# The adjacency of a graph network read for four tiles at a time, in pieces of 512 bytes, and its masks made one pair earlier

## The chip, the cores and the metric

The kernel runs on one core of one Trainium2 chip. The metric is the device time in microseconds (us), the median of the runs shown; lower is better. The core has five engines: TensorE (PE; the load of its weights is listed apart as PEld), VectorE (DVE), ScalarE (ACT), GpSimd (POOL) and SyncE (SP). Here SP issues the loads and POOL the stores; both are carried out by the core's 16 DMA engines.

## The reference

Two layers of a graph neural network on 2708 nodes with 1024 features, float32, with one adjacency matrix `adj` (2708 x 2708, int32, some 1% ones):

```python
# layer 0
h = jnp.maximum(_layernorm(x), 0.0)
f = h @ Wf + bf
g = h @ Wg + bg
e = jax.nn.relu(f @ g.T)
scores = jnp.where(adj > 0, e, NEG)          # NEG = -9e15
x = x + jax.nn.softmax(scores, axis=1) @ (h @ W + bW)
# layer 1
h = jnp.maximum(_layernorm(x), 0.0) @ W1
e = jax.nn.leaky_relu(h @ a1 + (h @ a2).T, 0.2)
e = jnp.where(adj > 0, e, NEG)
x = x + jax.nn.relu(jax.nn.softmax(e, axis=1) @ h)
```

Both layers need the mask of `adj`: 0 where there is an edge, a large negative number where there is none.

## The kernel before, in words

The rows of the score matrix are worked off in five panels `p`, of 576, 576, 532, 512 and 512 rows (`width`). Scores are held transposed: the neighbours are on the 128 partitions, the panel's rows run along the free dimension. The neighbours are cut into 20 full tiles of 128, taken as 10 pairs `q`, and what is left over (two partial tiles, MONO and TINY) is an eleventh unit, LEFT. Every full tile consists of four runs of 32 nodes that lie 128 apart; the two tiles of a pair are neighbours in `adj`, so that a row of it holds 64 consecutive numbers (256 bytes) for a pair in each of four places.

The large products are done with seven half-size products in place of eight (M1 to M7, Strassen's scheme in Winograd's form). For layer 0, `f @ g.T` is folded into `h @ (Wf Wg^T) @ h.T`: for each panel `project_q` makes the left side B, and `scores(p, B)` (L1382 to L1512) multiplies it with the tiles of `h`, which come as tiles `As` from `hs_d`, a buffer in DRAM. In panel 0 the tiles for it are only just being made: `make_until(q + 2)` sees to the units that the loop needs next, from x by way of `hsT`, whose parts are stored to `hs_d` by POOL. Then follow softmax, `aggregate` (the attention times `h`), and `project` with W; the panels follow each other, with the next panel's `project_q` between its scores and the aggregation of the one before.

The masks are made in panels too, by the three functions that `mask_maker(p)` returns (L783 to L840). `fetch(q)` loads the pair's adjacency: four DMAs into `adj_i`, each of 32 partitions x 16 blocks x 256 bytes (512 KB in all), and, in panels 0 to 2 whose width is over 512, four more into `adj_t` for the panel's tail of up to 64 rows. `convert(q)` turns the integers into bf16 values 0 or minus a large number, `nm`, in one VectorE operation, or two on ACT (`by_act`: the loop of panels 1 to 4). `turn(q, k)` turns the 32x32 squares of one tile with VectorE's transpose into its half of `mask`, and with k = 1 stores the pair's mask to `mk_d`, from where layer 1 reads it. `finish` (in `scores`) takes `mask` for layer 0 from the on-chip memory.

The pair's work is spread over the loop of `scores`. In step q stand `fetch(q + 2)` (L1436 to L1437), `convert(q + 1)` after product M5, `turn(q + 1, 0)` after M2 and `turn(q + 1, 1)` after M7. What a panel needs before its loop is made by `first_masks(p, step)` (L844 to L853), which is hung into the products ahead of it: those of `project_q` for panel 0 (M1, M2, M7), of `project` for panels 1 to 3 (M1, M5, M7) and of `aggregate` for panel 4 (M2, M6, M7).

What sets the order: `load` (L137) issues every load on SP in program order, so a load that has to wait holds up those behind it. `store` (L141) issues on POOL. SP's DMAs use eight completion semaphores in turn. `adj_i`, `As`, `x`, `w` and `hc` are taken in order from one ring of 12 stream buffers (`stream`, L127), and a buffer is free when the last reader of its former content, a store included, is done; `adj_t`, `nm`, `mask` and the score tiles come from 54 slots (`slot`). In the scores VectorE keeps the order of the program (`nc.hold`). Work of other stages is dealt out between products by `behind(rate)`.

Of the kernel before, what the change touches and what calls it, by code (L numbers as in the profile page):

```python
# [9 lines left out]
BF = mybir.dt.bfloat16  # L10
I32 = mybir.dt.int32
# [7 lines left out]
P = 128  # L19
W = 512  # L20
B32 = 32
# [36 lines left out]
def kernel(  # L58
# [19 lines left out]
    nc = InOrder(tc)  # L78
# [12 lines left out]
    F = W // P  # L91
# [20 lines left out]
    LEFT = NQ  # L112
    units = pairs + [(MONO, TINY)]
    order_of_units = [(q, k) for k in range(2) for q in range(NQ)] + [(LEFT, 0), (LEFT, 1)]
    WX, HX = width[0], width[0] // 2
# [9 lines left out]
    def slot(name, shape=(P, WX), dt=FP):  # L125
        return slots.tile(list(shape), dt, tag="slot", name=name)

    def stream(name, shape=(P, D), dt=FP):
        return strm.tile(list(shape), dt, tag="strm", name=name)

    def in_16(o, i):

        n = o.shape[0]
        k = n // 16 * 16
        return [(o, i)] if n in (k, 1) or not k or i.shape[0] != n else [(o[:k], i[:k]), (o[k:], i[k:])]

    def load(o, i):  # L137
        for a, b in in_16(o, i):
            tc.keep_in_program_order(nc.sync.dma_start(a, b))

    def store(o, i):  # L141
        for a, b in in_16(o, i):
            nc.gpsimd.dma_start(a, b)  # L143

    def bank(name, shape=(P, W), dt=FP):
        return psum.tile(list(shape), dt, tag="bank", name=name)
# [26 lines left out]
    mk_d = [dram.tile([P, NQ + 1, 2, width[p]], BF, name=f"mk_d{p}") for p in range(NP)]  # L173
# [109 lines left out]
    def add(o, a, b):  # L283
        nc.vector.tensor_tensor(o, a, b, OP.add)
# [91 lines left out]
    def sums_h():  # L376

        def fetch(q, two):
            i, j = group_of[q]
            for m in (M1, M2):  # L380
                two.append(stream("hr", (P, 2, W)))
                (load if "m" in got else by_scalar)(two[-1], hg_d[i][:, m:m + 2, j])

        def first(q, two):
            (a0, a1), (b0, b1) = ((t[:, 0], t[:, 1]) for t in two)
            add(b1, a1, b1)
            sub(a1, a0, a1)

        def second(q, two):
            (a0, a1), (b0, b1) = ((t[:, 0], t[:, 1]) for t in two)  # L390
            sub(a0, b1, a0)
            sub(b0, b0, a0)
            i, j = group_of[q]
            store(hg_d[i][:, M6:M7 + 1, j], two[0])
            store(hg_d[i][:, M3, j], b0)
            store(hg_d[i][:, M5, j], b1)
            summed[0] += 1
        for q in range(NQ):
            two = []
            put(1.4, lambda q=q, two=two: held(first, q, two), lambda q=q, two=two: fetch(q, two), ready=lambda: sums_may[0])  # L400
            put(1.4, lambda q=q, two=two: held(second, q, two), ready=lambda: sums_may[0])
# [34 lines left out]
    c0 = consts.tile([P, 1], FP, name="c0")  # L436
# [98 lines left out]
    def make_until(q):  # L535
        while min(q, NQ - 1) not in made:
            one()
# [113 lines left out]
    for name, gs in (("pick_lo", (0, 1)), ("pick_hi", (0, 2, 3))):  # L651
        t = consts.tile([P, P], FP, name=name)
# [128 lines left out]
    mk_sb = {}  # L781

    def mask_maker(p):  # L783

        r0, w = base[p], width[p]
        NG, NB = P // B32, W // B32
        tail = -(-(w - W) // B32)
        raw, neg = {}, {}

        def columns(q):  # L790

            if q < LEFT:
                return [[start_of_tile(t) + P * g for g in range(NG)] for t in pairs[q]]
            return [[base[g // 2] + W + g % 2 * B32 for g in range(NG)], [base[2] + W] * NG]

        def fetch(q):
            a = stream("adj_i", (P, NB, 2, B32), I32)
            b = slot("adj_t", (P, tail, 2, B32), I32) if tail else None
            raw[q] = a, b
            c0, c1 = columns(q)  # L800

            def square_rows(t, blocks, g, k, r, j, n):
                load(t[B32 * g:B32 * (g + 1), :, k] if k is not None else
                     t[B32 * g:B32 * (g + 1)].rearrange("p b k c -> p b (k c)"),
                     adj[r:r + blocks * B32, j:j + n].rearrange("(b r) j -> r b j", r=B32))
            for t, blocks, r in ((a, NB, r0), (b, tail, r0 + W)):
                for g in range(NG if t is not None else 0):
                    if q < LEFT:
                        square_rows(t, blocks, g, None, r, c0[g], 2 * B32)
                    else:  # L810
                        for k, c in enumerate((c0, c1)):
                            square_rows(t, blocks, g, k, r, c[g], B32)

        def convert(q, by_act=False):
            a, b = raw.pop(q)
            neg[q] = []
            for t, blocks in ((a, NB), (b, tail)):
                if t is not None:
                    m = slot("nm", (P, 2, blocks, B32), BF)
                    if by_act and t is a:  # L820
                        nc.scalar.activation(m, t.rearrange("p b k c -> p k b c"), AF.Sign, bias=minus_half)
                        nc.scalar.activation(m, m, AF.Identity, bias=minus_big, scale=BIG / 2)
                    else:
                        nc.vector.tensor_scalar(m, t.rearrange("p b k c -> p k b c"), 0.0, -BIG, op0=OP.is_le, op1=OP.mult)
                    neg[q].append(m)

        def turn(q, k):
            if k == 0:
                mk_sb[p, q] = slot("mask", (P, 2, WX), BF)
            mk = mk_sb[p, q]  # L830
            m = neg[q]
            nc.vector.transpose(mk[:, k, :W].rearrange("p (s g r) -> p g s r", s=F, g=NG),
                                m[0][:, k].rearrange("p (g s) c -> p g s c", g=NG))
            if tail:
                nc.vector.transpose(mk[:, k, W:W + tail * B32].rearrange("p (b r) -> p b r", r=B32), m[1][:, k])
            if k == 1:
                neg.pop(q)
                store(mk_d[p][:, q], mk[:, :, :w])

        return fetch, convert, turn  # L840

    makers = [mask_maker(p) for p in range(NP)]

    def first_masks(p, step):  # L844
        fetch, convert, turn = makers[p]
        if step == 0:
            fetch(0)
            fetch(1)
        elif step == 1:
            convert(0)  # L850
        else:
            turn(0, 0)
            turn(0, 1)  # L853

    def load_mask(p, q, k):
        mt = slot("maskl", (P, WX), BF)
# [525 lines left out]
    def scores(p, B):  # L1382

        w = width[p]
        h = w // 2
        lo, hi = slice(0, h), slice(h, w)
        fetch, convert, turn = makers[p]
# [44 lines left out]
        for q in range(NQ):  # L1432
            n = P
            make_until(q + 2)
            rate = 1.3 if NQ - 1 not in made else rates[p]
            if q + 2 <= LEFT:  # L1436
                fetch(q + 2)  # L1437
            if p == 0 and q == NQ - 2:
                ahead[0] = 2
                sums_h()  # L1440
            if p in ORDERED and q in (2, 6):
                (copy_residual if q == 2 else bias_residual)(p)
            sa, sb = slot("Sa"), slot("Sb")
            S[pairs[q][0]], S[pairs[q][1]] = sa, sb
            X, Y, Z = (bank(f"s{k}") for k in "xyz")
            m1, t = slot("sm1"), slot("st")
            product(q, M1, X, True)
            for s in (lo, hi):
                add(m1[:n, s], X[:n, :h], rb[:n, s])
            if left_over:  # L1450
                left_over()
            product(q, M6, Z, True)
            add(t[:n, lo], Z[:n, :h], m1[:n, hi])
            behind(rate, True)
            product(q, M5, Y, True)
            add(t[:n, hi], Y[:n, :h], m1[:n, hi])
            if q + 1 <= LEFT:
                convert(q + 1, p > 0)
            behind(rate, True)
            product(q, M2, X, False)  # L1460
            add(sa[:n, lo], X[:n, :h], rb[:n, lo])
            if q + 1 <= LEFT:
                turn(q + 1, 0)
            behind(rate, True)
            product(q, M7, Z, False)
            add(sb[:n, hi], Z[:n, :h], t[:n, hi])
            if q + 1 <= LEFT:
                turn(q + 1, 1)
            behind(rate, True)
            product(q, M3, Y, False)  # L1470
            add(sa[:n, hi], Y[:n, :h], t[:n, lo])
            finish(q, sa, 0)
            behind(2 * rate, True)
            left_over = lambda q=q, sb=sb, Z=Z, m1=m1: last(q, sb, Z, m1)
# [6 lines left out]
        t = stream("As", (P, 2, NH, P))  # L1481
# [408 lines left out]
    for p in range(NP):  # L1890
# [6 lines left out]
        g = aggregate_quartered(p, S, sm, next_right, then, fine=1.0) if p else aggregate(1, p, S, sm, then, rate=4.0)  # L1897
# [34 lines left out]
```

## Time and profile before

| | |
|---|---|
| Median of 3 runs | 3057.45 us (3056.61 to 3057.47) |
| The profiled execution | 3054.54 us |
| Its span, first to last instruction | 3052.8 us |
| Mean granted TensorE clock | 0.996 |
| TensorE busy | 3000.2 us, 98% of the span |
| VectorE / ScalarE / GpSimd busy | 67% / 18% / 16% |
| DMA | 766.80 MB in 448065 packets, mean 251 GB/s |
| Packets under 512 bytes | 175488 |
| `adj_i` loads of 128 KB on SP | 200 |
| Scores of panel 0 | from 210 to 379 us |

How to read it: the span is cut up by engine. A row such as "PE sx L1407 <- DMA As<-hs_d" says that TensorE, before the instruction of line 1407 that writes `sx`, stood idle until the DMA that loads `As` from `hs_d` had landed. The tiles are called by the program's names. Idle time of an engine that is not the bottleneck costs nothing by itself. The windows give, for a stretch of time, the busy time of each engine, the granted clock, and the share of the 16 DMA engines' time that was taken.

### The profile page before, as it was taken

Reading aid. Unit: us, or ns where it says so; the run is one execution under the profiler, and the core shown is the slowest. Engines: PE = TensorE matmul, PEld = TensorE weight load, DVE = VectorE, ACT = ScalarE, POOL = GpSimd, SP = SyncE. Lnnn points to the kernel's source line nnn. Section 1 sums busy time; section 2 is a strip of 40 time slices with the busy share of each in tenths; the row PEclk is TensorE's granted clock in tenths of the full one; section 3 lists DMA queues with packets and bytes.
Section 4 is the critical chain, followed back from the end, with each engine's and each line's share of the span. In section 5 each row is a group of like instructions: output and inputs, shape, how many; then the busy total and the mean of one; then the engine's idle time right before and its main releaser. Section 6 shows DMA issues by size and latency. Waiting matters only on the chain.

```text
span 3052.8 us, 41716 instructions
## 1 busy us (share of the span) xinstructions
PE 3000.2 (98%) x14642; PEld 2297.9 (75%) x14642; DVE 2043.3 (67%) x4578; ACT 545.6 (18%) x888; POOL 495.9 (16%) x770
## 2 busy tenths in 40 slices
PE   8999999999999999999999999999999999999999
PEld 5576777667877588885888886784767959879695
DVE  5776794575751586616965276867978768887863
ACT  3420020021200121101211011302222131212200
POOL 1421111210112110214111011131212010020201
PEclk9999999999999999999999999999999999999999
DMA  6989978887466786757967588689768768878797
GB/s 227 304 259 271 302 274 306 263 276 237 159 237 156 226 255 218 250 156 245 281 204 256 164 232 274 220 295 340 240 211 261 268 207 292 291 267 295 256 304 269
DMA packets 448065, 766.80 MB, mean 251 GB/s; under 512 B 175488, under 2 KB 262304, under 8 KB 447824
## 3 DMA queue, kind: packets, MB, share of 16 engines
q1 hardware_dynamic: 387696, 584.80, 59.7%
q0 software_dynamic: 54464, 164.78, 16.2%
q10 hardware_dynamic: 5696, 14.55, 1.4%
q8 instruction: 116, 1.90, 0.2%
q14 instruction: 93, 0.76, 0.1%
HBM read 630.04 MB, written 138.11 MB: 252 GB/s over the span
## 4 chain that ended last, share of the span: by engine, by line
PE 70%; issue 12%; DVE 11%; DMA 3%; POOL 2%; ACT 1%; SPq 1%; POOLq 0%; DVEq 0%; ACTq 0%
PE gy L678 6%; PE gz L678 6%; PE gz L1096 5%; PE sz L1407 5%; PE gx L678 5%; PE pz L1296 4%; PE px L1296 4%; PE py L1296 3%; PE sx L1407 3%; PE sy L1407 3%; PE gx L1096 3%; PE gy L1096 3%; PE M_ps L591 3%; PE gv L678 3%; DVE P L45 2%
## 5 line engine op out<-in xcount | busy, mean ns | idle before, releaser
L1407 PE MATMUL sz<-B,As 128*128 128x288 f32 (+2 forms) x1200 | 292.9, 393 | 6.9 <-DVE st L45 4.5
L1407 PEld LDWEIGHTS sz<-B,As 128*128 128x128 f32 x1200 | 227.8, 190 | 56.5 <-DVE st L45 8.0
L1407 PE MATMUL sx<-B,As 128*128 128x288 f32 (+2 forms) x800 | 202.6, 397 | 7.5 <-DMA As<-hs_d 5.6
L1407 PE MATMUL sy<-B,As 128*128 128x288 f32 (+2 forms) x800 | 199.9, 393 | 0.5 <-DMA As<-hs_d 0.5
L678 PE MATMUL gz<-Sa,hc 128*128 128x288 f32 (+2 forms) x800 | 185.8, 392 | 0.0
L1407 PEld LDWEIGHTS sx<-B,As 128*128 128x128 f32 x800 | 153.3, 192 | 41.8 <-issue 4.6
L1407 PEld LDWEIGHTS sy<-B,As 128*128 128x128 f32 x800 | 152.3, 191 | 31.9 <-DMA As<-hs_d 0.9
L678 PEld LDWEIGHTS gz<-Sa,hc 128*128 128x128 f32 x800 | 151.6, 190 | 32.2 <-issue 2.2
L1096 PE MATMUL gz<-quarter,hc 128*128 128x128 f32 (+2 forms) x1344 | 168.8, 279 | 3.8 <-DVE gT L45 3.7
L1096 PEld LDWEIGHTS gz<-quarter,hc 128*128 128x128 f32 x1344 | 160.6, 191 | 5.0 <-DVE gT L45 4.5
L143 POOL DMA_DIRECT2D out_dram<-x_res x164 | 80.9, 500 | 470.8 <-DVE x_res L45 460.6
L1296 PE MATMUL py<-w,ps 128*128 128x512 f32 x320 | 142.1, 593 | 0.4 <-DMA w<-wt_d 0.4
L1296 PE MATMUL pz<-w,ps 128*128 128x512 f32 x320 | 142.0, 594 | 0.0
L1296 PE MATMUL px<-w,gT 128*128 128x512 f32 x320 | 141.1, 593 | 0.0
L143 POOL DMA_DIRECT2D mk_d<-mask x55 | 35.9, 653 | 516.3 <-DVE mask L45 510.4
L1296 PEld LDWEIGHTS pz<-w,ps 128*128 128x128 f32 x320 | 60.2, 190 | 76.2 <-issue 71.9
L678 PE MATMUL gy<-T,hc 128*128 128x288 f32 (+2 forms) x480 | 113.6, 398 | 3.9 <-DMA hc<-hg_d 3.9
L1296 PEld LDWEIGHTS py<-w,ps 128*128 128x128 f32 x320 | 60.4, 190 | 75.8 <-issue 71.9
L1296 PEld LDWEIGHTS px<-w,gT 128*128 128x128 f32 x320 | 60.1, 190 | 71.3 <-issue 66.9
L591 PE MATMUL M_ps<-wgT,wfT 128*128 128x512 f32 x256 | 111.8, 593 | 1.6 <-ACT hsT L45 1.6
L678 PEld LDWEIGHTS gy<-T,hc 128*128 128x128 f32 x480 | 92.2, 192 | 24.4 <-DMA hc<-hg_d 4.4
L45 ACT ACTIVATE P<-P 128x576 f32<-128x576 f32 (+3 forms) x111 | 72.0, 650 | 207.3 <-DVE P L45 207.2
(391 smaller groups left out, 5830.6 us busy)
## 6 DMA issues: line engine op xcount, KB each, us to landing
hc<-hg_d SPq DMA_DIRECT2D x175, 512.0 KB
As<-hs_d SPq DMA_DIRECT2D x150, 512.0 KB
hc<-hr_d SPq DMA_DIRECT2D x119, 512.0 KB
hc<-hs_d SPq DMA_DIRECT2D x112, 512.0 KB
w<-wt_d SPq DMA_DIRECT2D x96, 512.0 KB
w<-in_L_gnn_W_dram SPq DMA_DIRECT2D x72, 512.0 KB
md<-md_d SPq DMA_DIRECT2D x56, 512.0 KB
adj_i<-in_adj_dram SPq DMA_DIRECT2D x200, 128.0 KB
```

The costliest lines, as they stand in the source:

```text
L45: i = f(*a, **k)
L143: nc.gpsimd.dma_start(a, b)
L591: nc.tensor.matmul(ps, wfT[a][c // NH][:, c % NH, :], wgT[b][c], start=(c == 0), stop=(c == NC - 1))
L678: nc.tensor.matmul(ps[d], left(m, k, d), right(m, k), start=(start and k == 0), stop=(k == K - 1), skip_group_check=True)
L1096: nc.tensor.matmul(ps[:, d], lhs[:, d * P:(d + 1) * P], inner_right(m, n, k), start=(start and k == 0 and d == 0), stop=(k == NK - 1), ski ...
L1296: nc.tensor.matmul(ps, left[i][m][:, k, :], w_[k], start=(start and k == 0), stop=(k == NH - 1), skip_group_check=True)
L1407: nc.tensor.matmul(ps[:n, :h], lefts[q][:, i % 2, c, :n], B[m][c // 2][:, c % 2, :h], start=(start and c == 0), stop=(c == NH - 1), skip_g ...
```

## The change

A unit n below LEFT is no longer a pair but half of the panel's first 512 rows (n even: the first 256; n odd: the others) for four tiles, the pairs n - n % 2 and the next one. A row of `adj` holds 128 consecutive numbers, 512 bytes, for them in each of the four places, so a fetch has four DMAs of 32 partitions x 8 blocks x 512 bytes, again 512 KB. The tail is loaded with odd n, for four tiles at once. `convert` has as many elements as before, with a tail in odd n alone, which is twice as wide. `turn(n, j)` fills half of the rows of the two tiles of one pair, in two transposes of 128x256 in place of one of 128x512, and with odd n does the tail as well. The masks of two pairs are complete after the odd unit and are stored then. LEFT is done as before.

All of it stands one pair further ahead: step q of the loop fetches unit q + 3 and converts and turns unit q + 2. `first_masks` therefore makes two units: step 1 converts and turns unit 0 and fetches unit 2, step 2 converts and turns unit 1. Over a panel the same bytes are read, converted and turned. Since one more unit is converted ahead of the loop, panels 1 to 4 have nine conversions by ACT in place of ten.

```diff
-        def fetch(q):
-            a = stream("adj_i", (P, NB, 2, B32), I32)
-            b = slot("adj_t", (P, tail, 2, B32), I32) if tail else None
...
+        def fetch(n):
+            parts = NG if n < LEFT else 2
+            h = n % 2 if n < LEFT else 1
+            nb = NB // 2 if n < LEFT else NB
+            a = stream("adj_i", (P, nb, parts, B32), I32)
+            b = slot("adj_t", (P, tail, parts, B32), I32) if tail and h else None
+            raw[n] = a, b
+            c0, c1 = columns(n // 2 * 2 if n < LEFT else n)
...
-            for t, blocks, r in ((a, NB, r0), (b, tail, r0 + W)):
+            for t, blocks, r in ((a, nb, r0 + (h * W // 2 if n < LEFT else 0)), (b, tail, r0 + W)):
                 for g in range(NG if t is not None else 0):
-                    if q < LEFT:
-                        square_rows(t, blocks, g, None, r, c0[g], 2 * B32)
+                    if n < LEFT:
+                        square_rows(t, blocks, g, None, r, c0[g], P)
...
-        def turn(q, k):
-            if k == 0:
-                mk_sb[p, q] = slot("mask", (P, 2, WX), BF)
-            mk = mk_sb[p, q]
-            m = neg[q]
-            nc.vector.transpose(mk[:, k, :W].rearrange("p (s g r) -> p g s r", s=F, g=NG),
-                                m[0][:, k].rearrange("p (g s) c -> p g s c", g=NG))
...
+        def squares(mk, k, m, at, gs):
+            nc.vector.transpose(mk[:, k, :W].rearrange("p (s g r) -> p g s r", s=F, g=NG)[:, gs],
+                                m[0][:, at].rearrange("p (g s) c -> p g s c", s=F))
+            if tail and len(m) > 1:
+                nc.vector.transpose(mk[:, k, W:W + tail * B32].rearrange("p (b r) -> p b r", r=B32), m[1][:, at])
+
+        def turn(n, j):
+            m = neg[n]
...
+                h, q = n % 2, n // 2 * 2 + j
+                if h == 0:
+                    mk_sb[p, q] = slot("mask", (P, 2, WX), BF)
+                for k in range(2):
+                    squares(mk_sb[p, q], k, m, 2 * j + k, slice(2 * h, 2 * h + 2))
+                done = h == 1
+            if j == 1:
+                neg.pop(n)
+            if done:
+                store(mk_d[p][:, q], mk_sb[p, q][:, :, :w])
...
         if step == 0:
             fetch(0)
             fetch(1)
-        elif step == 1:
-            convert(0)
-        else:
-            turn(0, 0)
-            turn(0, 1)
+            return
+        convert(step - 1)
+        turn(step - 1, 0)
+        turn(step - 1, 1)
+        if step == 1:
+            fetch(2)
...
-            if q + 2 <= LEFT:
-                fetch(q + 2)
+            if q + 3 <= LEFT:
+                fetch(q + 3)
...
-            if q + 1 <= LEFT:
-                convert(q + 1, p > 0)
+            if q + 2 <= LEFT:
+                convert(q + 2, p > 0)
...
-            if q + 1 <= LEFT:
-                turn(q + 1, 0)
+            if q + 2 <= LEFT:
+                turn(q + 2, 0)
...
-            if q + 1 <= LEFT:
-                turn(q + 1, 1)
+            if q + 2 <= LEFT:
+                turn(q + 2, 1)
```

More of the change, by code (lines that the diff above doesn't have):

```diff
@@ L794, in columns, with square_rows @@
             return [[base[g // 2] + W + g % 2 * B32 for g in range(NG)], [base[2] + W] * NG]
-        def fetch(q):
-            a = stream("adj_i", (P, NB, 2, B32), I32)
-            b = slot("adj_t", (P, tail, 2, B32), I32) if tail else None
-            raw[q] = a, b
-            c0, c1 = columns(q)
-            def square_rows(t, blocks, g, k, r, j, n):
+        def fetch(n):
[6 more added lines that the diff above has]
+            c0, c1 = columns(n // 2 * 2 if n < LEFT else n)
+            def square_rows(t, blocks, g, k, r, j, m):
                 load(t[B32 * g:B32 * (g + 1), :, k] if k is not None else
                      t[B32 * g:B32 * (g + 1)].rearrange("p b k c -> p b (k c)"),
-                     adj[r:r + blocks * B32, j:j + n].rearrange("(b r) j -> r b j", r=B32))
-            for t, blocks, r in ((a, NB, r0), (b, tail, r0 + W)):
+                     adj[r:r + blocks * B32, j:j + m].rearrange("(b r) j -> r b j", r=B32))
+            for t, blocks, r in ((a, nb, r0 + (h * W // 2 if n < LEFT else 0)), (b, tail, r0 + W)):
                 for g in range(NG if t is not None else 0):
-                    if q < LEFT:
-                        square_rows(t, blocks, g, None, r, c0[g], 2 * B32)
+                    if n < LEFT:
+                        square_rows(t, blocks, g, None, r, c0[g], P)
                     else:
@@ L812, in fetch, with convert @@
                             square_rows(t, blocks, g, k, r, c[g], B32)
[L814 to L817, printed above, removed]
+        def convert(n, by_act=False):
+            a, b = raw.pop(n)
+            neg[n] = []
+            for t in (a, b):
                 if t is not None:
-                    m = slot("nm", (P, 2, blocks, B32), BF)
+                    blocks, parts = t.shape[1:3]
+                    m = slot("nm", (P, parts, blocks, B32), BF)
                     if by_act and t is a:
@@ L824, in convert @@
                         nc.vector.tensor_scalar(m, t.rearrange("p b k c -> p k b c"), 0.0, -BIG, op0=OP.is_le, op1=OP.mult)
-                    neg[q].append(m)
-        def turn(q, k):
-            if k == 0:
-                mk_sb[p, q] = slot("mask", (P, 2, WX), BF)
-            mk = mk_sb[p, q]
-            m = neg[q]
-            nc.vector.transpose(mk[:, k, :W].rearrange("p (s g r) -> p g s r", s=F, g=NG),
-                                m[0][:, k].rearrange("p (g s) c -> p g s c", g=NG))
[L834 to L838, printed above, removed]
+                    neg[n].append(m)
+        def squares(mk, k, m, at, gs):
[5 more added lines that the diff above has]
+            m = neg[n]
+            if n == LEFT:
+                if j == 0:
+                    mk_sb[p, n] = slot("mask", (P, 2, WX), BF)
+                squares(mk_sb[p, n], j, m, j, slice(0, NG))
+                q, done = n, j == 1
+            else:
+                h, q = n % 2, n // 2 * 2 + j
[8 more added lines that the diff above has]
+                store(mk_d[p][:, q], mk_sb[p, q][:, :, :w])
         return fetch, convert, turn
```

## The prediction

> **What bounds the kernel now.** I read the page first: the busy times say what can be won at all, then who stands before whom.
>
> ```profile
> span 3052.8 us, 41716 instructions
> PE 3000.2 (98%) x14642; PEld 2297.9 (75%) x14642; DVE 2043.3 (67%) x4578; ACT 545.6 (18%) x888; POOL 495.9 (16%) x770
> DMA packets 448065, 766.80 MB, mean 251 GB/s; under 512 B 175488, under 2 KB 262304, under 8 KB 447824
> ```
>
> TensorE is busy for 3000.2 of 3052.8 us, and the change touches no matmul (in the built program its order is the same). So at most 52.6 us of idle time, and whatever slow clock that brings, is to be had. The list of TensorE's waits says where the idle time stands:
>
> ```profile
> PE sx L1407 <- DMA As<-hs_d: 5.6, 3, 2.8
> ...
> PE sz L1407 <- DVE st L45: 4.5, 6, 1.5
> ...
> PE sx L1486 <- DMA As<-hsl_d: 2.3, 1, 2.3
> PE sz L1407 <- DMA As<-hs_d: 2.3, 1, 2.3
> ...
> PE py L1296 <- DMA w<-wt_d: 0.4, 1, 0.4
> ```
>
> Columns: total, times, longest. The four DMA rows, with 0.5 more at sy, are waits for transfers that share the 16 DMA engines with the adjacency. By TensorE's timeline all but the `w` row fall in the scores of panel 0 (210 to 379 us):
>
> ```profile
> 237.78 3.14 PE L1407 MATMUL sz<-B,As 128*128 128x288 f32 x8 [2.32 <-DMA As<-hs_d]
> 240.72 2.87 PE L1407 MATMUL sy<-B,As 128*128 128x288 f32 x8
> 246.10 2.29 PE L1407 MATMUL sx<-B,As 128*128 128x288 f32 x4 [2.52 <-DMA As<-hs_d]
> 279.51 3.87 PE L1407 MATMUL sx<-B,As 128*128 128x288 f32 x8 [2.78 <-DMA As<-hs_d]
> ```
>
> Call the stalls A (237.78), B (246.10), C (279.51): 7.62 us. Around them groups of eight matmuls take 3.14, 2.87, 3.66 and 3.87 us where 2.10 is usual, 5.1 us more, at a lower granted clock. The windows show that clock, and the DMA engines full:
>
> ```profile
> 170.00:190.00 20.00, 20.00 (x84) 15.66 (x83) 8.13 (x18) 3.37 (x7) 2.85 (x6) 1.00 0.75 250
> 190.00:210.00 20.00, 20.00 (x95) 16.00 (x93) 14.85 (x31) 3.87 (x7) 3.76 (x7) 1.00 0.83 271
> 210.00:230.00 20.00, 20.00 (x94) 15.90 (x92) 16.45 (x42) 4.42 (x10) 4.51 (x8) 1.00 0.95 232
> 230.00:250.00 20.00, 15.16 (x58) 11.14 (x57) 15.55 (x38) 5.10 (x9) 4.86 (x9) 0.83 0.91 324
> 250.00:270.00 20.00, 20.00 (x93) 15.99 (x92) 16.74 (x38) 2.05 (x4) 3.44 (x6) 1.00 1.00 246
> 270.00:290.00 20.00, 17.22 (x64) 12.93 (x63) 9.49 (x20) 0.00 (x0) 0.55 (x1) 0.91 0.91 248
> ```
>
> The last three columns are clock, DMA share, GB/s. From 210 to 290 the share is 0.91 to 1.00. The wait list of SP's queue for 195 to 370 tells why As is late:
>
> ```profile
> SPq L139 <- DMA hs_d<-hsT: 23.4, 4, 11.3
> SPq L139 <- DMA hg_d<-hr: 17.3, 4, 10.1
> ```
>
> SP stands up to 11.3 us for a stream buffer whose last content must first be stored; those stores land that late because the engines are full. So two things bound A, B and C in series: the stores' landing and the DMA rate under it.
>
> [...] 342 GB/s per full share from 379 to 641 (284 / 0.83, almost no adj), 306 from 641 to 780 (248 / 0.81). [...] Here a stall of 2.3 us already brought slow groups.
>
> **The change part by part.**
> *Packets.* The 139 us from 641 to 780 at 0.81 are 1801 engine-us; 28.4 MB of other traffic at 21.4 B/ns (342 / 16) take 1327, which leaves 474 for some 26000 small packets: 18 ns each. A fetch with its tail has 2304 of them: 42 engine-us, 2.6 us of all 16 engines. At 21.4 B/ns a 512-byte piece takes 24 ns at best, [...] with its share of tail a fetch becomes 27 to 33 engine-us. Saved: 0.6 to 0.95 us of the full engines per step. In panel 0 that counts. In panels 1 to 4 TensorE doesn't wait for As at all, so 6 to 8 us of DMA time per panel are hidden there by TensorE itself; bare, they would be worth that much.
>
> *Lookahead.* Fetch, convert and transposes move one pair forward. SP issues fetch(2) of panel 0 before the x loads, 16 adj DMAs ahead of these as before (8+8, then 8+4+4), and one fetch per step from there. Into the time before A goes one more fetch: 4 x 32 = 128 engine-us against 3 x 42 = 126, the same load, partly in the slack of 170 to 210 (share 0.75 to 0.83). Steps with even n issue 4 adj DMAs instead of 8 (no tail). SP's DMAs share 8 semaphores in turn, so today each As load of panels 0 to 2 also waits for its own step's adj_i; that falls away in every other step. At q = 8 no fetch is left, so the last As and the hsl load of panel 0 get stream buffers of earlier contents and not those whose hg_d stores take 10.1 us: the stalls at 355.66 (0.49) and L1486 (2.33) should mostly go. The row at `w` (0.42; M5's load queues behind 16 adj DMAs) may go too.
>
> *A, B, C.* From 209 to 279 five fetches, each 0.6 to 0.95 us cheaper: 3 to 4.8 us of the 7.62; I take 4. The slow groups follow in proportion, 4 / 7.62 x 5.1 = 2.7. Sum 6.7.
>
> *VectorE.* A 128x512 transpose takes 0.70 us (0.62 from start to start), a 128x64 0.167, so a 128x256 about 0.395 (0.34). A step has four of these instead of two large: 1.36 against 1.24, +0.12; with tails even steps lose 0.3 to 0.5 and odd ones gain 0.2 to 0.4. Each panel has one convert (0.683) moved from ACT (2 x 1.148) to VectorE in panels 1 to 4, since two units are now converted before the scores, and eight transposes there: +1.1 us at M2 or M5, +1.15 at M7. The page has VectorE at 67%, and gaps of 0.4 to 2.9 us stand there (606 to 645). In panel 0 TensorE reuses the M3 banks at 184.59 while their eviction starts at 182.52: about 1.7 us of margin, 1.1 of it used. Without that cover the additions would cost 2.3 us per panel. TensorE's stalls behind VectorE at the starts of panels 1 to 3 sum to 6.4 us (for example 1.55 at 664.96, 1.49 at 1437.33), so a little will show: bounds 0 and 11, I take 1.3.
>
> *The rest.* Mask stores go in pairs: POOL is 16% busy and masks are needed only much later, in layer 1. Masks live one or two slots longer in mid-stage; the peak at the stage's end is the same.
>
> Sum: -6.7 (A, B, C) - 2.2 (80% of 2.82 at the panel's end) - 0.4 (`w`) + 1.3 = -8.0 us. The profiled execution took 3054.54 (span 3052.8, 1.7 outside it), so 3046.5 by its count; the runs' median is 3057.45, 2.9 higher, so I forecast 3049.5.
>
> **Rivals.** *The stalls stay.* The chain x load, hsT, its store, stream buffer, As sets A to C, and the store's landing hangs on latency more than on rate. For: SP stood 11.3 us for one store while the moved traffic was 232 GB/s; the load before A is the same. Against: stores elsewhere land sooner. Then -3 to 0, 3055 or so.
> *All goes.* The queue drains for good: 7.6 + 5.1 + 2.8 + 0.4 = 16, less 0 to 1 on VectorE: 3041 to 3042. Against: one convoy of stores suffices for a stall.
> *Slower: VectorE before the scores.* The two converts and eight transposes don't fit into the gaps, and evictions of the projection's banks run late, so TensorE waits for a bank. Place: M5 to M7 ahead of each panel and the first two pairs of scores. Price: 2.3 us x 5 = 11.5, with slow groups after it up to 15, less what A to C give back (about 6): +5 to +9, 3064. It decides where the free time of VectorE between M5 and the first product is under 2.3 us; in panel 1 it is over 14 us in total, but broken up, in panel 0 under 2.
> *The packets aren't cheaper.* The pieces do become 512 B; [...] it falls into the first rival.
>
> **How the numbers follow.** Forecast (-4 to -12): 0.41. All goes: 0.11. Stalls stay: 0.27. VectorE or another new wait: 0.21. A change under 0.2% (6.1 us) can't be told from none here. Faster by more: most of the forecast (0.36), nearly all of full recovery, a little of the others: 0.50. Slower by more: most of the VectorE case, 0.19. The rest, 0.31, is within. The range runs from full recovery (3040) to the VectorE case (3064); the forecast's own range is 3045 to 3054.
>
> **What would show it.** Packets under 512 B should fall by about 109,000; 128x256 transposes should average some 0.395 us. Right: no stall of over 1 us at L1407 behind As between 230 and 285, DMA share there under 0.9, SP's wait for hs_d stores under 12 us, no wait at L1486. Wrong by the first rival: the same stalls with a lower share. Wrong by VectorE: rows "<-DVE" at L1296 or L1407 growing by 2 us or more per panel at 180 to 190, 620 to 680 and 1080 to 1110. The forecast would also fail if the earlier fetch(2) made the first As or x late, shown by a new stall of TensorE at 200 to 235.

## The result, and the profile after

The changed kernel takes 3050.7 us (median of 15 runs, 3045.0 to 3056.59), the kernel before 3058.89 in the same comparison (15 runs, 3055.09 to 3065.61). The ratio is 0.9973, with a 95% interval of 0.9966 to 0.998: 6 to 10 us faster, 8.2 by the medians. The forecast was 3049.5.

The profiled execution doesn't show it. It took 3055.39 us and its span is longer than that of the kernel before. From the page of the kernel after:

```profile
span 3053.6 us, 41717 instructions
PE 2999.1 (98%) x14642; PEld 2300.7 (75%) x14642; DVE 2048.9 (67%) x4667; ACT 536.5 (18%) x880; POOL 495.2 (16%) x770
DMA packets 392704, 766.78 MB, mean 251 GB/s; under 512 B 65728, under 2 KB 206944, under 8 KB 392464
```

The packets under 512 bytes fell by 109,760 (forecast: about 109,000), the bytes stayed. The list of TensorE's waits of the kernel after:

```profile
PE sx L1424 <- DMA As<-hs_d: 9.3, 1, 9.3
PE sz L1424 <- DVE st L45: 5.2, 7, 1.3
```

L1424 is the former L1407. The rows for `hsl_d`, for `w<-wt_d` and for As at sz and sy are gone. But the wait for As at sx is now 9.3 us, in one piece, where A, B and C together were 7.6. TensorE's timeline:

```profile
247.86 4.21 PE L1424 MATMUL sx<-B,As 128*128 128x288 f32 x8 [9.29 <-DMA As<-hs_d]
```

So one stall stands at B's place, and at those of A and C there is none. The windows of the same stretches of time as before:

```profile
210.00:230.00 20.00, 20.00 (x93) 16.03 (x92) 16.80 (x43) 5.25 (x11) 3.97 (x7) 1.00 0.86 244
230.00:250.00 20.00, 10.71 (x50) 8.27 (x49) 14.88 (x39) 4.27 (x8) 5.38 (x10) 0.84 0.91 311
250.00:270.00 20.00, 20.00 (x85) 15.69 (x84) 13.91 (x32) 2.05 (x4) 2.90 (x5) 0.90 0.95 261
270.00:290.00 20.00, 20.00 (x85) 15.66 (x84) 13.20 (x31) 0.00 (x0) 1.09 (x2) 1.00 0.96 288
```

From 230 to 290 the DMA share is 0.91 to 0.96, hardly lower than before. And what SP waited for from 195 to 370 us, in the kernel after:

```profile
SPq L139 <- DMA hs_d<-hsT: 39.0, 7, 11.5
...
SPq L139 <- DMA hg_d<-hr: 6.1, 2, 4.3
```

The waits for stores of hsT grew from 23.4 to 39.0 us, those for hg_d fell from 17.3 to 6.1. To see which of this pays, one has to take the execution apart. TensorE's matmuls come in the same order in both kernels, so the time between the starts of the same two matmuls can be compared in every trace. The stages bear the times of the first profile of before; us, with TensorE's idle time in brackets. "Again" is a second execution of the same kernel.

| stage | before | before again | after | after again |
|---|---|---|---|---|
| 195 to 300, panel 0 scores | 105.1 (7.6) | 107.1 (9.9) | 104.4 (9.3) | 104.3 (9.4) |
| 345 to 379, its last steps | 34.3 (2.8) | 35.6 (2.8) | 31.2 (0.1) | 31.5 (0.2) |
| 606 to 641, project | 34.4 (0.4) | 35.0 (0.4) | 34.3 (0.0) | 34.3 (0.0) |
| 641 to 780, panel 1 scores | 139.0 (2.7) | 139.0 (2.8) | 139.2 (2.9) | 139.2 (2.9) |
| 1400 to 1530 | 129.9 (2.9) | 129.2 (2.2) | 130.3 (3.3) | 129.7 (2.7) |
| 1530 to 1860 | 330.0 (0.3) | 330.0 (0.3) | 329.4 (0.0) | 329.4 (0.0) |
| 1860 to 2215, end of layer 0, start of layer 1 | 355.1 (5.5) | 355.6 (5.9) | 357.9 (8.0) | 357.7 (6.1) |
| whole execution | 3054.54 | 3058.75 | 3055.39 | 3055.01 |

The means of the two say: -1.7 (panel 0), -3.6 (its end), -0.4 (`w`), +0.2 and +0.4 (VectorE), -0.6 (a last wait for As at 1841.80): -5.7 us. The row from 1860 to 2215, which the change hardly touches (the last mask is made at its start), gave 2 to 3 us back in the two executions of after, but spread from 353 to 358 over the runs below; the two executions of after also lie 2 to 5 us over that kernel's median. Two stages that are not listed, and that the change doesn't touch directly, gave back another 1.0 us (379 to 606) and 0.9 us (from 2215 on). So a page against a page says "no gain", stage by stage a gain is plain in panel 0 and at its end, and some 2 us of the 8.2 are not located.

### The profile page after: what moved, and what is told of

It is laid out like the page before. It is cut to its first block, busy times and chain, and to the rows that moved or that the text cites. A ratio compares the mean times of both kernels' runs of the same rounds, so it can differ in the third digit from the quotient of the medians.

```text
span 3053.6 us, 41717 instructions
## 1 busy us (share of the span) xinstructions
PE 2999.1 (98%) x14642; PEld 2300.7 (75%) x14642; DVE 2048.9 (67%) x4667; ACT 536.5 (18%) x880; POOL 495.2 (16%) x770
## 4 chain that ended last, share of the span: by engine, by line
PE 70%; issue 12%; DVE 11%; DMA 4%; POOL 2%; ACT 1%; SPq 0%; POOLq 0%; DVEq 0%; ACTq 0%
PE gy L678 6%; PE gz L678 6%; PE sz L1424 5%; PE gz L1113 5%; PE gx L678 5%; PE pz L1313 4%; PE px L1313 4%; PE sy L1424 3%; PE sx L1424 3%; PE gx L1113 3%; PE M_ps L591 3%; PE py L1313 3%; PE gy L1113 3%; PE gv L678 3%; DVE P L45 2%
## 5 line engine op out<-in xcount | busy, mean ns | idle before, releaser
L1424 PE MATMUL sz<-B,As 128*128 128x288 f32 (+2 forms) x1200 | 292.9, 393 | 5.4 <-DVE st L45 5.2
L1424 PEld LDWEIGHTS sz<-B,As 128*128 128x128 f32 x1200 | 228.3, 191 | 54.5 <-DVE st L45 8.4
L1424 PE MATMUL sx<-B,As 128*128 128x288 f32 (+2 forms) x800 | 201.3, 395 | 11.0 <-DMA As<-hs_d 9.3
L1424 PE MATMUL sy<-B,As 128*128 128x288 f32 (+2 forms) x800 | 199.0, 392 | 0.0
L1424 PEld LDWEIGHTS sx<-B,As 128*128 128x128 f32 x800 | 152.8, 192 | 44.0 <-DMA As<-hs_d 9.7
L1424 PEld LDWEIGHTS sy<-B,As 128*128 128x128 f32 x800 | 152.0, 190 | 30.4 <-DVE st L45 0.3
L591 PE MATMUL M_ps<-wgT,wfT 128*128 128x512 f32 x256 | 112.7, 597 | 1.6 <-ACT hsT L45 1.6
```

The costliest lines, as they stand in the source:

```text
L591: nc.tensor.matmul(ps, wfT[a][c // NH][:, c % NH, :], wgT[b][c], start=(c == 0), stop=(c == NC - 1))
L1424: nc.tensor.matmul(ps[:n, :h], lefts[q][:, i % 2, c, :n], B[m][c // 2][:, c % 2, :h], start=(start and c == 0), stop=(c == NH - 1), skip_g ...
```

## The experiments

Times are given as the ratio to the kernel before on the same chip, with the 95% interval; at 3059 us, 0.001 is 3.1 us.

**The changed kernel again, and the kernel before again.**

> The changed kernel once more, for a second profiled execution. In the first one the stalls of TensorE behind As in panel 0 came to 9.3 us in one piece (at 247.86) with slow groups after it, no less than the 7.6 us of the kernel before, and the gain up to 2160 us was 4.3 us, while the medians differ by 8.2. Theory 1 (the forecast: cheaper packets shorten the stalls behind As): a typical execution has much less, 3 to 5 us of stall between 230 and 285. Theory 2 (the stalls between 230 and 285 only move; the gain is the panel's end): 7 to 10 us again, and a time near 3053. Time by both: 0.9973 of the kernel before.

> The kernel before once more, for a second profiled execution: its median over all runs is 3059.8, and the execution profiled first took 3054.5, so that one should be no typical one. If panel 0 is where executions differ, the stalls behind As between 230 and 285 now come to more than 7.6 us (10 to 12 with the execution at 3058 to 3061); if they are 7.6 again, the spread lies elsewhere.

After again: 0.9976 (0.9966 to 0.9986), stall 9.44 at 249.91. The forecast's 3 to 5 us of stall don't occur; theory 2 is right on the stall and, with a median of 3053.15 us in this comparison, on the time. Before again took 3058.75 us, and its timeline of TensorE has

```profile
246.40 3.77 PE L1407 MATMUL sx<-B,As 128*128 128x288 f32 x8 [6.02 <-DMA As<-hs_d]
281.33 4.18 PE L1407 MATMUL sx<-B,As 128*128 128x288 f32 x8 [3.84 <-DMA As<-hs_d]
368.72 3.90 PE L1486 MATMUL sx<-B,As 128*128 128x288 f32 x8 [2.79 <-DMA As<-hsl_d]
```

Here A is already part of B, and the total between 230 and 285 is 9.9, not 7.6. The execution on which the forecast rested was a lucky one. The stall of the hsl product has 2.3 to 3.1 us in every execution without the lookahead. The group of eight behind it is slow in three of these five (3.65 to 3.90 us) and takes 2.21 us in the two others.

**The change in halves.** The lookahead alone, with pairs and 256-byte pieces (against the kernel before; conversion and transposes move as in the change):

```diff
+        if step == 1:
+            fetch(2)
...
-            if q + 2 <= LEFT:
-                fetch(q + 2)
+            if q + 3 <= LEFT:
+                fetch(q + 3)
...
```

> The kernel before with the lookahead alone: fetch, convert and transposes one pair further ahead, pieces of 256 bytes and pairs as before. Theory 1 (pieces): only the panel's end and the w load gain, -2.5 to -3.5 us; the stalls between 230 and 285 stay at 7 us or more. Theory 2 (order): nearly all of the gain, -6 to -9 us. Both: no stall at the hsl product (2.33 before).

1.0005 (0.9996 to 1.0014): no gain, and both theories missed, each of which expected one. Its end of panel 0 is as good as the changed kernel's (31.6 us, no stall at the hsl product), but 195 to 300 takes 112.7 us, 6 to 8 more than before. TensorE's timeline:

```profile
220.42 3.81 PE L1408 MATMUL sy<-B,As 128*128 128x288 f32 x8 [2.57 <-DMA As<-hs_d]
253.69 4.21 PE L1408 MATMUL sx<-B,As 128*128 128x288 f32 x8 [8.30 <-DMA As<-hs_d]
288.79 3.76 PE L1408 MATMUL sx<-B,As 128*128 128x288 f32 x8 [3.88 <-DMA As<-hs_d]
```

The first of these is new. It is the failure that the prediction named last: fetch(2) makes As late. SP's timeline for the lookahead alone:

```profile
189.85 7.32 SPq L139 DMA_DIRECT2D x<-in_x_dram  x16
197.27 2.97 SPq L139 DMA_DIRECT2D adj_i<-in_adj_dram  x4
200.35 3.46 SPq L139 DMA_DIRECT2D adj_t<-in_adj_dram  x4
203.97 1.11 SPq L139 DMA_DIRECT2D As<-hs_d  x1
205.18 10.40 SPq L139 DMA_DIRECT2D x<-in_x_dram  x16
```

24 DMAs of adjacency (8 each for units 0, 1 and 2) now stand before the first x loads of that row, which begin at 189.85; in the changed kernel there are 16, and they begin at 182.95. The second x loads begin at 205.18 instead of 195.07.

The other half, four-tile units and 512 bytes with the old lookahead (against the changed kernel; `first_masks`, conversion and transposes go back as well):

```diff
...
-            if q + 3 <= LEFT:
-                fetch(q + 3)
+            if q + 2 <= LEFT:
+                fetch(q + 2)
...
```

> The changed kernel with the lookahead of before: half panels, pieces of 512 bytes, four tiles at a time, but fetch(q+2), convert(q+1) and turn(q+1) in step q, and one unit ahead of the loop. Theory 1 (pieces): -4 to -7 us, the stalls between 230 and 285 down by half, the stall at the hsl product still about 2.3. Theory 2 (order): 0 to -2 us.

0.9986 (0.9979 to 0.9993), -4.3 us: just inside the first theory's range. But the stalls between 230 and 285 were not halved (7.9 us). 195 to 300 takes 103.5 us, some 2.6 less than the two executions of before, and another 2.2 us are gained where neither theory expected it: 641 to 780 takes 136.8 us instead of 139.0, with waits for VectorE of 1.0 instead of 2.7. The panel's end stays as in the kernel before:

```profile
365.08 2.21 PE L1502 MATMUL sx<-B,As 128*128 128x288 f32 x8 [3.07 <-DMA As<-hsl_d]
```

So the two halves don't add up. Without the new units the lookahead costs 1.5 us (within its interval nothing), with them it gains 3 to 4 (0.9986 to 0.9973 or 0.9976; these intervals overlap a little, but the panel's end alone shows 3.5). In panel 1 the lookahead takes away again what the units alone had won there (139.2 us); why is open.

**Is it the packets?** The same kernel as after, with panel 0's adjacency (`adj_i`) in pieces of 4096 bytes, and in pieces of 256, with equal numbers of DMAs and bytes:

```diff
-                    if n < LEFT:
+                    if n < LEFT and p == 0 and t is a:
+                        load(t[B32 * g:B32 * (g + 1)].rearrange("p b k c -> p (b k c)"),
+                             adj[r + B32 * g:r + B32 * (g + 1), P * n:P * n + blocks * P])
+                    elif n < LEFT:
                         square_rows(t, blocks, g, None, r, c0[g], P)
```

```diff
-                    if n < LEFT:
+                    if n < LEFT and p == 0 and t is a:
+                        load(t[B32 * g:B32 * (g + 1)].rearrange("p b k c -> p (b k c)").rearrange("p (b j) -> p b j", j=P // 2),
+                             adj[r0:r0 + W, c0[g]:c0[g] + P // 2].rearrange("(b r) j -> r b j", r=B32))
+                    elif n < LEFT:
                         square_rows(t, blocks, g, None, r, c0[g], P)
```

> The changed kernel with panel 0's adjacency read in pieces of 4096 bytes: the same number of DMAs and of bytes, from other places of adj, so that panel 0's masks are made from wrong numbers (their tail excepted). Theory 1 (time of the packets): 8 packets of 512 bytes take 264 engine-ns in the trace of after, one of 4096 takes 194, so that a step saves 1024 x 33 - 128 x 194 = 9 engine-us, as much again as 256 to 512 did: -2 to -5 us against the changed kernel. Theory 2 (number and order of DMAs, not their packets): within 1 us of the changed kernel.

> The changed kernel with panel 0's adjacency read in pieces of 256 bytes, 16 row blocks by 64 numbers: number and order of DMAs and their bytes as in the changed kernel, tail as there; panel 0's masks are made from wrong numbers. Theory 1 (time of the packets): +3 to +5 us against the changed kernel, the stall of step 2 at 10 or more, C back. Theory 2 (number and order of DMAs, the tail's halved count above all): within 1 us of the changed kernel.

4096 bytes: 0.998 (0.997 to 0.9989). 256 bytes: 0.9981 (0.9972 to 0.999). Neither differs from the other, nor, within the intervals, from the changed kernel. The stage is the sharper measure: 195 to 300 takes 103.8 us with 4096 bytes and 102.5 with 256, against 104.4 and 104.3. The packets are cheaper as expected: in the traces' packet records one of 256 bytes takes 20 ns on average over the kernel before, one of 512 takes 33 over the kernel after, one of 4096 about 194. The windows 195:300 of the changed kernel, of the one with 4096 bytes and of the one with 256:

```profile
195.00:300.00 105.00, 95.71 (x414) 75.23 (x412) 79.53 (x188) 14.61 (x28) 17.64 (x32) 0.95 0.91 276
```

```profile
195.00:300.00 105.00, 95.35 (x423) 75.21 (x422) 78.97 (x188) 15.44 (x29) 17.64 (x32) 0.95 0.86 263
```

```profile
195.00:300.00 105.00, 96.88 (x426) 75.91 (x425) 79.71 (x189) 15.39 (x29) 17.64 (x32) 0.98 0.93 283
```

The DMA share falls from 0.91 to 0.86 with 4096 bytes and rises to 0.93 with 256; TensorE's busy time stays, or even rises a little with 256. Between 230 and 250 TensorE idles for 7.8 us in two pieces there, not for the 10 us or more that theory 1 expected, and C doesn't come back. Theory 1 has fallen: in panel 0 of the changed kernel the time doesn't hang on what a packet costs. (In the order of the kernel before, pieces alone were not tried.)

**Is it the number of DMAs on SP?** The lookahead with pairs and 256 bytes, but the tail loaded for two pairs at once (half as many adj_t DMAs; the lookahead's own lines and the tail's bookkeeping are left out here), and the lookahead with fetch(2) of panel 0 moved to step 0 (against the lookahead alone):

```diff
...
-            b = slot("adj_t", (P, tail, 2, B32), I32) if tail else None
+            parts = NG if q < LEFT else 2
+            b = slot("adj_t", (P, tail, parts, B32), I32) if tail and (q % 2 == 0 or q == LEFT) else None
...
```

```diff
-        if step == 1:
+        if step == 1 and p > 0:
             fetch(2)
...
+            if p == 0 and q == 0:
+                fetch(2)
             if q + 3 <= LEFT:
                 fetch(q + 3)
```

> The lookahead (e1) with pairs, 256 bytes and full panel rows as before, but the tail loaded for two pairs at once, with even units: half as many adj_t DMAs, which is the third thing that the changed kernel does. Theory C (the number of DMAs on SP is what the four-tile units save): most of e1's loss of 6 us between 195 and 300 goes, the time comes to 3052 to 3056, 4 to 8 us under e1. Theory D (it is the halves of panel rows or the order of the masks): as e1, 3060 or more.

> The lookahead (e1) with panel 0's fetch(2) moved behind the x loads, to the start of step 0. Theory C (e1 loses because 8 more DMAs stand before the x loads, so that x, hsT and As all come late): the new stall at 220 us (2.57) goes and 195 to 300 us takes 106 or less, -5 to -7 us against e1. Theory E (two fetches in step 0 now stand before As instead): the loss only moves, 0 to -2 us against e1.

With the tail for two pairs: 0.999 (0.9983 to 0.9997), in theory C's range at its lower end: 4.6 us under the lookahead alone, 195 to 300 in 108.1 us, no stall at 220. Pairs and pieces of 256 bytes are kept for `adj_i` here (the tail's pieces become 512 bytes as its DMAs are halved), and this alone turns the loss into a gain. It doesn't reach the changed kernel (104.4); 20 DMAs stand before the x loads here, 16 there. What the rest is (those four, or the halves of the rows) was not separated.

With fetch(2) later: 1.0006 (0.9998 to 1.0014). The stall at 220 is gone, as theory C says, but 195 to 300 still takes 109.8 us, only 2.9 less than with the lookahead alone, stalls of 8.40 and 4.45 remain, and the time is that of the lookahead alone: theory E. Eight DMAs moved from before the x loads to before the As loads mostly move the wait. By SP's timelines, 24 DMAs of adjacency stand before panel 0's first As load in the kernels before and after and in the one with the tail for two pairs, and 32 in the two versions that lose.

**Where the adjacency stands among the As loads.** The changed kernel with fetch(q+3) behind the first As load of the step, and behind the second:

```diff
-            if q + 3 <= LEFT:
-                fetch(q + 3)
...
             if left_over:
                 left_over()
+            if q + 3 <= LEFT:
+                fetch(q + 3)
```

```diff
-            if q + 3 <= LEFT:
-                fetch(q + 3)
...
             product(q, M5, Y, True)
+            if q + 3 <= LEFT:
+                fetch(q + 3)
```

> The changed kernel with fetch(q+3) moved behind the first As load of the step and the last one of the step before, so that As no longer stands behind the adjacency on SP after the wait for a stored buffer. Theory 1 (SP's order after that wait makes As late): the 9.3 us stall of the first product of step 2 falls to 4 or 5, slow groups go with it, -3 to -6 us against the changed kernel. Theory 2 (the landing of the hs_d stores alone decides): the stall moves to the second or third load of the step, 0 to -1.5 us.

> As e5, with fetch(q+3) one product later still, behind the second As load of the step. If every As load gains that no longer stands behind the adjacency, and conversion a step later still finds its data: -1 to -3 us against e5, 3045 to 3047. If the adjacency now comes late for its conversion, or the third As load takes the wait: 0 to +3 us.

Behind the first: 0.9965 (0.9952 to 0.9977), -10.7 us. That is 2 to 3 under the changed kernel, with intervals that overlap; 195 to 300 takes 103.5 us, 0.9 less. The timeline of TensorE has the 9.3 us broken up:

```profile
241.42 2.21 PE L1424 MATMUL sx<-B,As 128*128 128x288 f32 x8 [2.48 <-DMA As<-hs_d]
255.51 2.18 PE L1424 MATMUL sz<-B,As 128*128 128x288 f32 x8 [2.09 <-DMA As<-hs_d]
269.73 3.15 PE L1424 MATMUL sy<-B,As 128*128 128x288 f32 x8 [4.28 <-DMA As<-hs_d]
```

The first product of step 2 waits 2.5 instead of 9.3, but stalls behind later loads come up, 8.9 us in all: theory 2's move, and a gain that is not clear of noise. Behind the second: 0.9942 (0.993 to 0.9954), -17.7 us, 3041.26 us, the fastest version here, some 10 under the changed kernel and better than was expected. One stall behind As is left:

```profile
242.74 4.21 PE L1424 MATMUL sx<-B,As 128*128 128x288 f32 x8 [3.81 <-DMA As<-hs_d]
```

195 to 300 takes 99.1 us, 5.2 less than in the changed kernel and half of the gain, at nearly the same DMA share:

```profile
195.00:300.00 105.00, 101.19 (x437) 79.21 (x436) 82.20 (x196) 14.98 (x29) 17.70 (x32) 0.97 0.90 273
```

In the kernel after, SP's timeline reads

```profile
236.39 2.06 SPq L139 DMA_DIRECT2D adj_i<-in_adj_dram  x4
238.49 2.86 SPq L139 DMA_DIRECT2D adj_t<-in_adj_dram  x4
241.47 10.18 SPq L139 DMA_DIRECT2D As<-hs_d  x4
```

SP comes free at 236.39, when the store that held the buffer has landed (POOL issued it at 226.44, it landed at 236.33), and issues eight DMAs of adjacency that nobody needs for a step. As follows at 241.47, and TensorE, idle since 238.57, gets it at 247.86. In the version with fetch behind the second load SP's timeline has

```profile
224.81 14.12 SPq L139 DMA_DIRECT2D As<-hs_d  x4
239.03 3.84 SPq L139 DMA_DIRECT2D adj_i<-in_adj_dram  x4
```

The As loads come first: the first row joins the last one of the step before (224.81) with three of this step, the first of which goes out at 236.87. TensorE starts its product at 242.74, 5.9 us later; in the changed kernel it is 6.4 us from 241.47 to 247.86. SP still waits 38.3 us for hs_d stores from 195 to 300, about as long as in the changed kernel (39.0): the wait was not removed, only what stands behind it was. This version is also 2.3 us shorter from 641 to 780 (waits for VectorE 1.1 instead of 2.9) and 1.2 shorter from 1400 to 1530; why is open.

**The end of panel 0.** First the left-over unit's fetch one step sooner in the kernel before, then its conversion and transposes too:

```diff
-            if q + 2 <= LEFT:
+            if q + 2 < LEFT:
                 fetch(q + 2)
+            if q + 3 == LEFT:
+                fetch(LEFT)
```

```diff
+            if q + 2 == LEFT:
+                convert(LEFT, p > 0)
...
+            if q + 2 == LEFT:
+                turn(LEFT, 0)
...
+            if q + 2 == LEFT:
+                turn(LEFT, 1)
```

> The kernel before with one edit: the left-over unit's adjacency is fetched one step sooner (in step 7 with that of unit 9, none in step 8), in all panels. It takes the stream buffers of step 8 out of the sequence just before the last As and the hsl load. Both theories: the stall of 2.33 at the hsl product and the 0.49 before it go, -2 to -3 us, everything before 300 us as it was. If that stall has another cause than the buffer's earlier content, it stays and the time is the same within 1 us.

> The kernel before with the left-over unit alone one step sooner, in all panels: its fetch in step 7, as in e4, and now its conversion and transposes in step 8 too. Theory A (what frees the stream buffer is the conversion, which reads adj_i: done in step 8 it gives the last loads of panel 0 a buffer, and hsl no longer waits for an hg_d store): 345 to 379 us takes 31 to 32 us instead of 34.3 to 35.6, the stall at the hsl product is gone, -3 to -4 us against the kernel before. Theory B (the stall's end hangs on the DMA traffic of the last steps): as e4, within 1 us of the kernel before.

The fetch alone: 0.9998 (0.9991 to 1.0006), and the stall at hsl is there with 2.94 us. Both theories missed. In the built program the buffer of the hsl load is still one whose former content, an hr tile, has to be stored to hg_d first; SP waits 17.2 us for such stores from 195 to 370. With the conversion too: 0.9994 (0.9987 to 1.0), and the view of SP's waits (310 to 375) has

```profile
SPq L139 <- DMA hg_d<-hr: 0.2, 1, 0.2
```

That part of theory A holds: it is the conversion in step 8, not the fetch, that frees a buffer for the last loads, and the wait for hg_d falls from 17.2 to 0.2. The stall stays all the same:

```profile
364.94 3.65 PE L1494 MATMUL sx<-B,As 128*128 128x288 f32 x8 [2.37 <-DMA As<-hsl_d]
```

In this build the scheduler has put the hsl product two products earlier, ahead of M7 and M3. Its load is issued at 356.57 and needed at 362.6, 6.0 us later; in the changed kernel it is issued at 351.78 and needed at 361.29, 9.5 us later. So the run shows what frees the buffer, and not that this makes the 3.6 us: in the changed kernel SP still waits 6.1 us for hg_d stores, and the stall is gone all the same. That the lookahead as a whole makes them is shown: 345 to 379 takes 31.2 to 32.0 us in all nine executions that have it, 34.3 to 35.6 in the five that haven't.

## Why the prediction was right, and where it was not

*Total.* 3049.5 was forecast, 3050.7 measured, and that waits for As in panel 0 and at its end hold what can be won is what the runs show. The working behind it is right in place in two small terms and wrong in its largest. Of the four signs that were to show it right, one came (no wait at the hsl product). The three others failed: a stall of 9.3 us stands between 230 and 285, the DMA share there is not under 0.9, and SP waits 39.0 us in all for hs_d stores, not under 12 (the longest wait, 11.5 us, is as long as before).

*Packets, and A, B, C (-6.7).* This step failed. Packets did get cheaper (40 to 33 ns for 512 bytes, 17% less; 36 to 24 at best was the author's estimate, from 18 ns a small piece and 21.4 B/ns), but neither 256 nor 4096 bytes move the time. The 18 ns came from a count of 26000 small packets from 641 to 780; the trace has 13824 of 256 bytes and 20672 in all under 512 there. The upper end of the 27 to 33 engine-us that a fetch was to take, and with it the 0.6 us saved per step, was the author's estimate; no trace had shown it. The stalls were to lose 4 of 7.62 us; they total 9.3. What the stage gained is 1.7 us. By the prediction's working its full-clock time is 92.4 us (105.14 less 7.6 of stall less 5.1 of slow groups); that leaves 5.1 and 4.8 us of slow clock in the two executions of before, 2.7 and 2.5 in those of after.

The rival "the stalls stay" was right on the stall and on its chain (stores landing, SP standing behind them); it erred in calling this the whole result. The prediction read a queue of DMAs as a rate: the full share of 0.91 to 1.00 was taken for the limit. What moves the time is SP's order, where As stands behind adjacency after a wait of 11 us: the run with the fetch behind the second As load takes 5.2 us off this stage at a DMA share of 0.90. The wait of 11 us itself was put down to full engines, which no run shows. The store that ends it lands 9.9 us after its issue in the changed kernel and 9.6 with pieces of 4096 bytes, so cheaper packets hardly shorten it; what makes it so long is open. That "stores elsewhere land sooner" holds for most: from issue to landing the medians over the kernel before are 4.4 to 5.9 us for `mk_d`, 4.7 for `x_d`, 6.1 and 5.8 for `hg_d<-hr`, and 6.9 for the stores of hsT themselves.

*Lookahead.* "The same load" before A was the right count for the changed kernel, but by the wrong measure. The prediction named the 16 DMAs ahead of the x loads and gave their number no price. With 24 there the lookahead alone loses 6 to 8 us in 195 to 300, and with 16 there, but 32 instead of 24 ahead of the first As load, it still takes 109.8. So DMAs ahead of x and DMAs ahead of As both cost; what each kind costs was not separated. SP's waits for its earlier loads didn't fall away either: from 195 to 370 it waited 2.4 us for `adj_i`, 2.2 for `adj_t` and 0.2 for As before, and 1.5, none and 11.0 after.

*End of panel 0 (-2.2) and `w` (-0.4).* Right in place, the first too small: -3.6, since the stall is 2.3 to 3.1, in some executions with slow groups behind it, and goes entirely. Its reason was off: moving the fetch away from q = 8 alone changes nothing, and with the conversion moved too the wait for hg_d goes but the stall stays. What in the lookahead ends the stall is open. `w`: -0.4.

*VectorE (+1.3).* Nearly nothing against the kernel before: +0.2 and +0.4 in the two stages where it shows. (Against the new units alone the lookahead costs 2.4 us in panel 1.) The 128x256 transposes average 416 ns (estimate 395), and TensorE has no wait of over 0.1 us from 160 to 205 in either kernel, so the work ahead of panel 0's scores finds its gaps. The price of the slower rival did not arise.

*The slower rival and the others.* No bank came late at 184.59. "All goes" would have needed the order of SP to change, and a kernel that changes it went 17.7 us down, beyond that rival's 16, though a part of that lies in panels which the rival did not name.

The right total is thus partly luck: 5 us too much for the packets, against 1.4 too little for the panel's end, 0.7 too much loss for VectorE, a gain of 0.6 in panel 4 that was not listed (the prediction had no wait for As behind panel 0; there was one of 0.3 at 1841.80), and some 2 us that two executions of each don't locate.

## What to carry to other kernels

When an in-order load queue stands for a buffer, ask what it issues first when it comes free: loads for later work belong behind the load that the bound engine needs next (here worth some 10 us of 3050, half of them in the stage itself). A full DMA share next to a stall isn't proof of a rate limit; change the packet size at an equal number of DMAs before believing it. And where executions differ by 0.3%, compare stages between two matmuls in several traces, not one page with another.

## What the runs showed of the hardware

- In panel 0 of the changed kernel, at an equal number of DMAs and bytes, adjacency in pieces of 4096, 512 and 256 bytes took a DMA share of 0.86, 0.91 (0.89 again) and 0.93 from 195 to 300, and the stage 103.8, 104.4 (104.3 again) and 102.5 us: no loss with the smaller pieces.
- How much slow clock follows a stall isn't set by its length here. Stalls of 2.32 and 2.78 us were followed by groups of eight of 3.14 and 3.87 us (2.10 is usual), but one of 2.48 us by 2.21 and one of 3.07 by 2.21; after 3.81 and after 9.29 us the group took 4.21 both times.
- SP issued the eight adjacency DMAs between 236.39 and 241.35 us in 4.96 us, 0.6 us each; a load behind them goes out that much later.
- Halving the number of small tail DMAs (32 partitions x 2 blocks, 256-byte pieces made 512) took 195 to 300 from 112.7 to 108.1 us and the time from 1.0005 to 0.999 (4.6 us; the intervals just touch) where they stood ahead of other loads on SP.
